# A graph layer on one core: window sums with carried overlaps, degree counts on two halves of the array, and tiles projected beside them

## The chip, the cores and the metric

The program runs on one core of a Trainium2 chip. The core has a matrix engine (PE in the profile; PEld is its weight load), a vector engine (DVE), a scalar engine (ACT), a general engine (POOL) and a queue engine (SP) that mostly issues transfers. The five follow their own instruction lists and meet at semaphores. The metric is the time of one execution in device microseconds (us), the median of the runs.

## The reference

There are 6250 nodes with 256 features and 200000 edges, which are sorted by their destination `dst`; many edges end at low node numbers, few at high ones. The reference does this:

```python
deg_out = clip(segment_sum(ones, src), 1)
deg_in  = clip(segment_sum(ones, dst), 1)
h  = feats * rsqrt(deg_out)[:, None]
m  = segment_sum(h[src], dst) * rsqrt(deg_in)[:, None]
x  = (m @ W_gc + b_gc) + (feats @ W_res + b_res)
core = moe(x)          # top 2 of 64 experts, 256 -> 512 -> 256, capacity 1024
y  = x + core          # then batch norm over the nodes, residual and layer norm
```

The change lies in all that comes before `x`, and in the one addition that forms `x`. The experts and the norms behind it stay as they are.

## The kernel before

**Projection first.** Since the sum over edges and `W_gc` commute, the kernel projects each of 50 tiles of 125 nodes with `W_gc` and `W_res` side by side (`wcat`, 512 columns): two transposes on PE into `pt` (L261), an ACT copy to `fT` (L263), two matmuls into `pr` (L266), ACT copies of the two halves to `y` (L267) and `xr` (L268). Per five tiles POOL adds the biases `bsum` to `xr` (L269), which is then written to `r_dram`.

**Degree counts.** `deg_out` is counted by matmuls. A source number is split into `hi = src // 125` and `lo = src % 125`. Edges stand in 1568 groups of 128, one edge per partition. For 32 groups at a time DVE makes the one-hot rows of `hi` (`hot_hi`, L233) and of `lo` (`hot_lo`, L237), as comparisons of two bf16 operands, and PE does one matmul per group into `degp`, 50 x 128 (L241). Both one-hot tiles have two buffers.

**Scaling and splitting.** With the counts there, `s_out` = 1/sqrt(degree) is formed. ACT scales `y` by it and rounds the result to the first half of `hrow` (L351); DVE puts what the rounding lost into the second half (L352). `hrow` is held on the chip and written to `h_dram` too, five tiles at a time on SP.

**Sums over edges.** The 1563 groups that hold edges are divided by a planner, `_plan()`. The first `GD` groups, where destinations are dense, form dense chunks of a tuple `(g0, k, w, n)`: `n` slots of `k` groups, each with at most `w` neighbouring destinations. For each group DVE makes a one-hot of `lo` (L410) and one of a combined key for (`hi`, slot position) (`hotk`, L414); PE multiplies them (L416), which counts how often each source meets each destination; ACT moves a slot's counts to `counts` (L418). When a chunk's counts are full, PE multiplies them with all 50 tiles of `hrow`, both halves (100 matmuls, L424 and L426). ACT copies the sums, and a one-hot matmul (`to`, L437, called spread) moves each sum to its place in a window of 128 nodes.
The other groups form gather chunks: POOL's indirect transfer fetches the 128 rows of a group from `h_dram` (L380) into a ring of `NR` = 10 buffers, DVE makes a one-hot of the destination within a window of 128 (`hot`, L383), and PE adds both halves (L384, L385) into the chunk's window.
Before, there are 35 dense chunks (997 groups) and 33 gather chunks (566 groups).
Windows of neighbouring chunks overlap, since a node's edges may stretch over two chunks. Each of the 68 windows is therefore added to `z_dram` by a POOL indirect transfer with addition (L361), some ten gathers after it was formed (`LAG`).

**What sets the order.** A scheduler orders the instructions of each engine by its own estimates, and the program's text sets what may pass what. In the sum phase the text runs both kinds of chunks side by side: before gather number `issued`, dense steps are taken until their planned cost reaches `share * (issued + 10)`. The `share` is the planned cost of all dense steps per gather, 648.9/566 = 1.146 before and 629.7/582 = 1.082 after. Counting only the costs that the steps themselves report (596 and 585), dense steps run out before gather 510 of 566, and in the changed kernel before gather 531 of 582.

**Keys.** The keys and tests which tell for every edge whether it fits its slot and window are made from `dst` and from tables of first destinations by some twenty POOL operations over 128 x 1568 or 128 x `GD` values (L294 to L334), with three of DVE (L325 to L327) that use `okd`, a flag that no degree is above 4096. Edges that fit nowhere are handled by a general loop behind the sum phase, which runs zero times for this input.

## Time and profile before

| quantity | value |
| --- | --- |
| median of 3 runs | 2521.09 us (2520.99 to 2524.98) |
| profiled execution | 2519.15 us, span from first to last instruction 2517.4 us |
| mean granted clock of PE | 0.847 |
| busy: PE, DVE, ACT, POOL | 1860.4, 1218.8, 543.8, 1151.8 us |
| first gather issued, last scatter issued | 468.45, 1382.76 us |
| bytes moved by transfers | 387.12 MB, mean 154 GB/s |

An instruction row reads: start, duration, engine, line, operation, output<-inputs, shape, count, and in brackets the idle time ahead of it with what ended it. A group row gives count, busy time, mean ns of one, and idle time with its releasers. A wait row gives the time waited in all, how often, and the longest. Ends of matmuls are modelled, so the distance of two starts says more than a duration. Matmuls on `hrow` are listed as f32.

### The profile page before, as it was taken

The page shows a single profiled execution, that of the slowest core. Times are in us where ns is not written, and L with a number is a line of the kernel's source. Part 1 is how long each engine was busy: PE and PEld are TensorE (multiplying, and loading weights), DVE is VectorE, ACT ScalarE, POOL GpSimd, SP SyncE. Part 2 cuts the span into 40 slices and gives each one's busy share as a digit, 9 for nine tenths or more (in the row PEclk, how much of TensorE's full clock was granted, in tenths as well). Part 3 has the DMA queues.
Part 4 walks back from the last instruction along what each step waited for, and adds up shares of the span by engine and source line. Part 5 has one row for each costly group of instructions (what it writes and reads, how often), then busy time and mean ns, then how long its engine had stood idle before and what let it go on. Part 6 is the DMA issues. An engine that isn't in the chain of part 4 may idle for free. (4 is left out here: it accounts for less than half of the span.)

```text
span 2517.4 us, 32629 instructions
## 1 busy us (share of the span) xinstructions
PE 1860.4 (74%) x10910; PEld 1413.1 (56%) x10910; DVE 1218.8 (48%) x4128; ACT 543.8 (22%) x1376; POOL 1151.8 (46%) x1097
## 2 busy tenths in 40 slices
PE   3808865989999999999884642679999999843340
PEld 3605421566777888878773530258888888730010
DVE  6907229766665555544431369931111112223368
ACT  0001224222433333333320210012222222310020
POOL 6992230476677777777767000022222222138800
PEclk9958985798899999999995555989999999975565
DMA  9501226376566666776676820057777777873314
GB/s 238 174 0 32 82 61 217 105 195 156 146 168 169 180 179 180 176 181 166 172 190 183 216 63 0 1 185 220 225 221 226 224 222 219 260 188 84 83 35 132
DMA packets 243599, 387.12 MB, mean 154 GB/s; under 512 B 29643, under 2 KB 172035, under 8 KB 243430
## 3 DMA queue, kind: packets, MB, share of 16 engines
q0 software_dynamic: 75360, 191.62, 29.7%
q1 hardware_dynamic: 128891, 153.92, 20.5%
q10 hardware_dynamic: 39179, 39.47, 5.5%
q8 instruction: 89, 1.46, 0.2%
q14 instruction: 80, 0.66, 0.1%
HBM read 304.86 MB, written 79.96 MB: 153 GB/s over the span
## 5 line engine op out<-in xcount | busy, mean ns | idle before, releaser
L380 POOL DMA_INDIRECT r<-h_dram,srcg x566 | 550.3, 972 | 222.6 <-issue 74.8
L424 PE MATMUL sm<-hrow,counts 125*126 125x258 f32 (+2 forms) x1750 | 436.9, 287 | 0.2
L426 PE MATMUL sm<-hrow,counts 125*126 125x256 f32 (+2 forms) x1750 | 434.5, 285 | 0.0
L679 POOL DMA_INDIRECT xg<-x_dram,ids x128 | 121.4, 948 | 619.7 <-PE pte L682 325.5
L383 DVE TENSOR_SCALAR hot<-iota_f,key 128x128 fp32r<-128x128 f32 x566 | 157.9, 303 | 397.0 <-PE pg L385 395.3
L424 PEld LDWEIGHTS sm<-hrow,counts 125*126 125x126 f32 (+2 forms) x1750 | 335.4, 192 | 1.1 <-issue 0.4
L426 PEld LDWEIGHTS sm<-hrow,counts 125*126 125x126 f32 (+2 forms) x1750 | 335.8, 192 | 0.0
L416 PE MATMUL pc<-hotk,lo 128*128 128x250 bf16 (+5 forms) x997 | 293.8, 329 | 49.0 <-DVE lo L410 25.3
L414 DVE TENSOR_SCALAR hotk<-iota_h,key 128x250 bf16<-128x250 f16 (+5 forms) x997 | 326.4, 330 | 0.0
L689 PE MATMUL ph<-xgT,w1s 128*128 128x256 f32 (+1 forms) x1280 | 274.8, 366 | 16.8 <-DVE xgT L684 16.8
L418 ACT CAST counts<-pc 128x350 fp32r<-128x350 f32 (+5 forms) x670 | 261.1, 489 | 111.8 <-PE pc L416 104.9
L410 DVE TENSOR_SCALAR lo<-iota_h,lo_f 128x128 bf16<-128x128 f16 x997 | 255.2, 257 | 25.1 <-PE pc L416 24.1
L696 PE MATMUL py<-w2s,hT 128*128 128x256 f32 x1152 | 262.0, 379 | 1.4 <-DVE ys L698 1.4
L689 PEld LDWEIGHTS ph<-xgT,w1s 128*128 128x128 f32 x1280 | 218.1, 190 | 63.1 <-DVE xgT L684 26.7
L698 DVE TENSOR_TENSOR ys<-py,b2s 128x256 f32<-128x256 f32 x144 | 60.9, 424 | 387.1 <-PE py L696 333.0
L384 PE MATMUL pg<-r,hot 128*128 128x258 f32 x566 | 199.4, 359 | 64.2 <-DMA r<-h_dram,srcg 48.1
L696 PEld LDWEIGHTS py<-w2s,hT 128*128 128x128 f32 x1152 | 217.5, 190 | 30.6 <-DVE ys L698 1.8
L691 ACT ACTIVATE hT<-ph,b1T 128x256 f32<-128x256 f32 x256 | 121.3, 474 | 364.2 <-PE ph L689 364.2
L416 PEld LDWEIGHTS <-lo 128*128 128x128 bf16 x997 | 91.9, 99 | 180.7 <-DVE hotk L414 75.3
L266 PE MATMUL pr<-wcat,fT 128*125 128x512 f32 x200 | 106.6, 667 | 97.8 <-ACT fT L263 97.8
L385 PE MATMUL pg<-r,hot 128*128 128x256 f32 x566 | 175.9, 316 | 0.0
L384 PEld LDWEIGHTS pg<-r,hot 128*128 128x128 f32 x566 | 114.7, 203 | 105.9 <-DVE hot L383 52.4
(219 smaller groups left out, 2180.2 us busy)
## 6 DMA issues: line engine op xcount, KB each, us to landing
w1s<-in_L_gnn_w_dram SPq DMA_DIRECT2D x80, 512.0 KB
w2s<-in_L_gnn_w_dram SPq DMA_DIRECT2D x80, 512.0 KB
y_dram<-ys SPq DMA_DIRECT2D x64, 256.0 KB
y_dram<-zeros ACTq DMA_DIRECT2D x1, 12416.0 KB
h_dram<-hrow SPq DMA_DIRECT2D x10, 1120.0 KB
b2s<-in_L_gnn_b_dram SPq DMA_DIRECT2D x80, 128.0 KB
r<-h_dram,srcg POOLq DMA_INDIRECT x566, 3.7
z_dram<-zeros ACTq DMA_DIRECT2D x1, 6321.0 KB
```

Source lines behind the costliest of these rows:

```text
L380: G.indirect_dma_start(out=f32(r[:, :2 * D]), out_offset=None, in_=h_dram[:, :], in_offset=bass.IndirectOffsetOnAxis(ap=idx, axis=0))
L383: V.tensor_scalar(hot, iota_f[:, :WIN], at, None, op0=ALU.is_equal)
L384: T.matmul(pg, hot, r[:, D:], start=first, stop=False)
L385: T.matmul(pg[:, :D], hot, r[:, :D], start=False, stop=last)
L410: V.tensor_scalar(lo, iota_h[:, :128], lo_f[:, g:g + 1], None, op0=ALU.is_equal)
L414: V.tensor_scalar(hot, iota_h[:, :NT * w], key[:, g:g + 1], None, op0=ALU.is_equal)
L416: T.matmul(pc, lo, hot, start=(i == 0), stop=(i == k - 1))
L418: S.copy(counts[:, :, j * w:(j + 1) * w], pc)
L424: T.matmul(sm[:m], counts[:TP, t, :m], hrow[:, t, D:], start=(t == 0), stop=False)
L426: T.matmul(sm[:m, :D], counts[:TP, t, :m], hrow[:, t, :D], start=False, stop=(t == NT - 1))
L689: T.matmul(ph[:, :m], w1s[:, kk, c * 128:(c + 1) * 128], xgT[:, kk, :m], start=(kk == 0), stop=(kk == 1))
L696: T.matmul(py, hT[:, c, k * 128:(k + 1) * 128], w2s[:, c, :], start=(c == 0), stop=(c == 3))
```

## The change

1. **Degree counts on two halves of the array.** `degp` has 128 partitions; even groups add into partitions 0 to 49, odd ones into 64 to 113 (L241, both before and after). The two halves are added when `s_out` is made.
2. **28 tiles projected beside them** (`EARLY`). They have no scale yet. ACT rounds the tile to `hrow` (L274), copies it unrounded to `whole` (L276, two buffers), and POOL writes the difference into `hrow`'s second half (L277). When `s_out` is known, POOL adds the two halves again (L358), and ACT (L251) and DVE (L252) scale and split anew. The remaining 22 tiles are projected after that and scaled straight from the accumulator `pr`. The buffer `y` and the pass over it are gone. Node tiles are read two at a time, not five, and `r_dram` is written from SP, not ACT. The bias addition moves to the stage that forms `x`.
3. **Keys.** A running maximum of the chunks' first destinations gives each window's base; ACT forms `mis` = `dst` - base in 68 pieces (L302, L303); the POOL operations follow on it (L315 to L338). `okd` is applied later, in `to` and in the general loop.
4. **Sweep with carried overlaps.** The windows of the dense chunks go upward, those of the gather chunks downward. Each window takes what its neighbour has for its nodes, by a one-hot matmul with the neighbour's copied result (`carried`, one-hot L424, `over`), and is then written over `z_dram` by a plain transfer on SP, whose row comes from a register (L431 to L433). POOL's 68 adding transfers go. The last dense window takes in both neighbours.
5. **One-hots of `lo` for eight groups at a time** (`PAIRS`) in the manner of the degree loop (L194), read by PE with a stride of two. `hotk` has ten buffers, not six; the ring of gathered rows has nine, not ten. The planner's costs change: 34 dense chunks (981 groups) and 34 gather chunks (582 groups).

The core of the diff:

```diff
+PAIRS = 8
+EARLY = 28
 FIRST = 256
 MORE = 2 * N // 128
 EXTRA = 16
-LAG = 10
...
     def cost(k, w, n):
-        return 13.0 + n * k * (0.06 + w * 0.0208)
+        return 13.5 + n * k * (0.04 + w * 0.0208)
 
     dense, g, pe = [], 0, 0.0
-
-    while pe + (NGU - g) * 0.33 < (NGU - g) * 1.25 + (len(dense) + 30) * 1.9:
+    while pe + (NGU - g) * 0.26 < (NGU - g) * 1.25 + 50.0:
...
-            c = cost(k, w, n) - 0.33 * n * k
+            c = cost(k, w, n) - 0.26 * n * k
...
-            srci = dp.tile([128, NGR], I32, name="srci")
-            nc.sync.dma_start(out=srci, in_=src)
-            dstf = dp.tile([128, NGR], F32, name="dstf")
-            G.dma_start(out=dstf, in_=dst)
-            mis = dp.tile([128, NGR], F32, name="mis")
-            G.dma_start(out=key, in_=bases[0:1, :].to_broadcast([128, NGR]))
-            G.dma_start(out=mis, in_=bases[1:2, :].to_broadcast([128, NGR]))
+            srcf = dp.tile([128, NGR], F32, name="srcf", tag="a")
+            G.dma_start(out=srcf, in_=src)
+            G.dma_start(out=key[:, :GD], in_=bases.to_broadcast([128, GD]))
+            first = dp.tile([128, NC], F32, name="first")
+            G.dma_start(out=first, in_=firsts.to_broadcast([128, NC]))
...
-                    T.matmul(degp, hot_hi[:, c // 2, :, c % 2], hot_lo[:, c // 2, :, c % 2],
-                             start=(c0 + c == 0), stop=(c0 + c == NGR - 1))
-
-
+                    r = c % 2
+                    T.matmul(degp[64 * r:64 * r + NT, :], hot_hi[:, c // 2, :, r],
+                             hot_lo[:, c // 2, :, r], start=(c0 + c < 2), stop=(c0 + c >= NGR - 2))
...
+            def halves(t, rows):
+
+                S.activation(hrow[:, t, :D], rows, AF.Copy, scale=s_out[:, t:t + 1])
+                V.scalar_tensor_tensor(hrow[:, t, D:2 * D], rows, s_out[:, t:t + 1],
+                                       f32(hrow[:, t, :D]), op0=ALU.mult, op1=ALU.subtract)
+                if t % 5 == 4:
+                    node_dma(nc.sync, False, f32(hrow[:, t - 4:t + 1, :2 * D]),
+                             node_rows(h_dram, t - 4, 5))
+
+            def project(t):
+                if t % 2 == 0:
+                    state["f"] = ld.tile([TP, 2, D], F32, name="f")
+                    node_dma(nc.sync, True, state["f"], node_rows(x_in, t, 2))
+                    state["xr"] = ld.tile([TP, 2, D], F32, name="xr")
+                f, xr = state["f"][:, t % 2, :], state["xr"]
+                pt = ps_a.tile([128, 2, TP], F32, name="pt")
+                for k in range(2):
+                    T.transpose(pt[:, k, :], f[:, k * 128:(k + 1) * 128], ident[:TP, :TP])
+                fT = ld.tile([128, 2, TP], F32, name="fT")
+                S.copy(fT, pt)
+                pr = ps_a.tile([TP, 2 * D], F32, name="pr")
+                for k in range(2):
+                    T.matmul(pr, fT[:, k, :], wcat[:, k, :], start=(k == 0), stop=(k == 1))
+                if t < EARLY:
+
+                    S.copy(hrow[:, t, :D], pr[:, :D])
+                    whole = ld.tile([TP, D], F32, name="whole")
+                    S.copy(whole, pr[:, :D])
+                    G.tensor_tensor(hrow[:, t, D:2 * D], whole, f32(hrow[:, t, :D]), ALU.subtract)
+                else:
+                    halves(t, pr[:, :D])
+                S.copy(xr[:, t % 2, :], pr[:, D:])
+                if t % 2:
+                    node_dma(nc.sync, False, xr, node_rows(r_dram, t - 1, 2))
...
+            for t in range(EARLY):
+                project(t)
...
+            V.tensor_tensor_scan(run, ones[:, :NC], first, 0.0, op0=ALU.mult, op1=ALU.max)
+            V.tensor_copy(base_i, run[0:1, :])
+            V.memset(shift, 0.0)
+            V.tensor_sub(shift[:, 1:ND], run[:, :ND - 1], run[:, 1:ND])
+            V.tensor_sub(shift[:, ND:NC], run[:, ND:NC], run[:, ND - 1:NC - 1])
+            V.tensor_scalar(shift, shift, pidx, None, op0=ALU.add)
+            neg = dp.tile([128, NC], F32, name="neg")
+            V.tensor_scalar(neg, run, -1.0, None, op0=ALU.mult)
+            mis = dp.tile([128, NGR], F32, name="mis", tag="b")
+            chunks = [(g0, k * n) for g0, k, w, n in DENSE] + GATHER
+            for c, (g0, k) in enumerate(chunks):
+                S.activation(mis[:, g0:g0 + k], dstf[:, g0:g0 + k], AF.Identity, bias=neg[:, c:c + 1])
...
+            G.tensor_tensor(key[:, :GD], dstf[:, :GD], key[:, :GD], ALU.subtract)
+            fit = dp.tile([128, NGR], BF16, name="fit")
+            t1 = dp.tile([128, NGR], BF16, name="t1")
+            G.tensor_scalar(fit, mis, 0.0, None, op0=ALU.is_ge)
+            G.tensor_scalar(t1, mis, float(WIN), None, op0=ALU.is_lt)
+            G.tensor_tensor(fit, fit, t1, ALU.mult)
...
+            V.tensor_copy(s_out, pd[:, :NT])
+            V.tensor_add(s_out, s_out, pd[:, 64:64 + NT])
...
+            for t in range(EARLY):
+                whole = ld.tile([TP, D], F32, name="whole")
+                G.tensor_tensor(whole, f32(hrow[:, t, :D]), f32(hrow[:, t, D:2 * D]), ALU.add)
+                halves(t, whole)
+            for t in range(EARLY, NT):
+                project(t)
...
-        for t in range(NT):
-            S.activation(hrow[:, t, :D], y[:, t, :], AF.Copy, scale=s_out[:, t:t + 1])
-            V.scalar_tensor_tensor(hrow[:, t, D:2 * D], y[:, t, :], s_out[:, t:t + 1],
-                                   f32(hrow[:, t, :D]), op0=ALU.mult, op1=ALU.subtract)
-            if t % 5 == 4:
-                node_dma(nc.sync, False, f32(hrow[:, t - 4:t + 1, :2 * D]),
-                         node_rows(h_dram, t - 4, 5))
...
-            NR = 10
+            NR = 9
...
-            def send(until):
-                while waiting and (until is None or waiting[0][0] <= until):
-                    _, res, idx = waiting.pop(0)
-                    add_to_nodes(res, idx)
+            def carried(pg, res, col, last):
+
+                to = rsp.tile([WIN, WIN], F32, name="over")
+                V.tensor_scalar(to, iota_f[:, :WIN], shift[:, col:col + 1], None, op0=ALU.is_equal)
+                T.matmul(pg, to, res, start=False, stop=last)
 
             def sums_done(pg, c):
...
-                res = rsp.tile([WIN, D + 2], F32, name="res", bufs=6)
+
+                res = rsp.tile([WIN, D + 2], F32, name="resd" if c < ND else "resg", bufs=2)
                 S.copy(res, pg)
-                waiting.append((issued + LAG, res, cidx[:, c:c + 1]))
+                row = nc.values_load(base_i[0:1, c:c + 1], engines=(SP_E,), min_val=0, max_val=N,
+                                     skip_runtime_bounds_check_because="at most N")
+                nc.sync.dma_start(out=z_dram[ds(row, WIN), :], in_=res)
+                return res
...
-                            lo = hc.tile([128, 128], BF16, name="lo")
-                            V.tensor_scalar(lo, iota_h[:, :128], lo_f[:, g:g + 1], None,
-                                            op0=ALU.is_equal)
+                            r = (g - g0) % PAIRS
+                            if r == 0:
+                                lo = hc.tile([128, PAIRS // 2, 128, 2], BF16, name="lo", bufs=3)
+                                hot_pairs(lo, lo_b, g, PAIRS, 128)
...
-                            T.matmul(pc, lo, hot, start=(i == 0), stop=(i == k - 1))
+                            T.matmul(pc, lo[:, r // 2, :, r % 2], hot, start=(i == 0), stop=(i == k - 1))
...
-                        T.matmul(pg, to[:m], sums[:m], start=True, stop=True)
-                        sums_done(pg, c)
-                spread()
-
-            steps, done = dense(), 0.0
+                        T.matmul(pg, to[:m], sums[:m], start=True, stop=(c == 0 and ND > 1))
+                        if c:
+                            carried(pg, ends_met["dense"], c, c < ND - 1)
+                        if c == ND - 1:
+                            carried(pg, ends_met["gather"], ND, True)
+                        ends_met["dense"] = sums_done(pg, c)
+                yield spread
...
+            for i, (g0, k) in reversed(list(enumerate(GATHER))):
                 pg = ps_g.tile([WIN, D + 2], F32, name="pg")
                 for g in range(g0, g0 + k):
-                    while steps is not None and done < share * (issued + 10):
-                        d = next(steps, None)
-                        if d is None:
-                            steps = None
+                    while finish is None and done < share * (issued + 10):
+                        d = next(steps)
+                        if callable(d):
+                            finish = d
                         else:
                             done += d
+                    alone = i == len(GATHER) - 1 and g == g0 + k - 1
                     gathered(pg, ring[issued % NR], srcg[:, g - GD:g - GD + 1], key[:, g:g + 1],
-                             g == g0, g == g0 + k - 1)
+                             g == g0, alone)
                     issued += 1
-                    send(issued)
-                sums_done(pg, ND + i)
-            for _ in steps or ():
-                pass
-            send(None)
+                if i < len(GATHER) - 1:
+                    carried(pg, ends_met["gather"], ND + i + 1, True)
+                ends_met["gather"] = sums_done(pg, ND + i)
+            while finish is None:
+                d = next(steps)
+                finish = d if callable(d) else None
+            finish()
...
             node_dma(nc.scalar, True, xr, node_rows(r_dram, t0, 5))
+            G.tensor_tensor(xr, xr, bsum[:, None, :].to_broadcast([TP, 5, D]), ALU.add)
             s_in = xl.tile([TP, 5], F32, name="s_in")```

Where instructions stand now. First POOL, between its last key operation and the first gathers (`r_...` are buffers of the ring). Before:

```order
L334 TENSOR_SCALAR mis<-mis 128x1568
L361 DMA z_dram<-res,cidx 6378x258
L380 DMA r_2956<-h_dram,srcg 128x512
L380 DMA r_2959<-h_dram,srcg 128x512
L380 DMA r_2962<-h_dram,srcg 128x512
```

After:

```order
L331 TENSOR_SCALAR key<-key 128x981
L337 TENSOR_SCALAR mis<-t_2648 128x587
L358 TENSOR_TENSOR whole<-hrow 125x256
L338 TENSOR_TENSOR mis<-mis,dstf 128x1568
L358 TENSOR_TENSOR whole<-hrow 125x256 x21
L414 DMA r_3184<-h_dram,srcg 128x512
L414 DMA r_3187<-h_dram,srcg 128x512
```

The scatter of the first dense window no longer stands ahead of the first gather; 21 of the 28 second additions now do, behind the key operations.

Second ACT, in the degree loop (tiles 2 and 3 of the projection). Before:

```order
L263 COPY fT<-pt 128x250 x2
L267 COPY y<-pr 125x256
L268 COPY xr<-pr 125x256
L267 COPY y<-pr 125x256
L268 COPY xr<-pr 125x256
```

After:

```order
L268 COPY fT<-pt 128x250 x2
L274 CAST hrow<-pr 125x256
L276 COPY whole<-pr 125x256
L280 COPY xr<-pr 125x256
L274 CAST hrow<-pr 125x256
L276 COPY whole<-pr 125x256
L280 COPY xr<-pr 125x256
```

Each tile has one ACT instruction more, and L276, which waits for POOL's subtraction of two tiles earlier, stands ahead of the next `fT`.

Third ACT after the degree loop, from the last small piece of `mis` to the first of the last sixteen tiles, in the changed kernel, with the rows between cut out at one place:

```order
L302 ACTIVATE mis<-dstf,neg 128x6
L353 ACT_TABLE_LOAD
L353 ACTIVATE s_out<-s_out 125x50
L314 ACTIVATE key<-mis 128x587
L251 ACTIVATE hrow<-whole,s_out 125x256 x2
L268 COPY fT<-pt 128x250 x2
...
L251 ACTIVATE hrow<-whole,s_out 125x256
L280 COPY xr<-pr 125x256 x2
L251 ACTIVATE hrow<-whole,s_out 125x256 x21
L268 COPY fT<-pt 128x250 x2
L251 ACTIVATE hrow<-pr,s_out 125x256
```

Between the small pieces and the 21 scalings only six tiles are projected; the other sixteen come behind the scalings, and so behind the POOL additions that these wait for.

226 lines of the change are left out of this document (100 added, 126 removed).

## The prediction

> **What bounds the kernel now.** I read the windows view first, cut at the borders of the stages, because the page's chain of waits begins only in the last 300 us. Columns: stretch, its length, then busy time of PE, PEld, DVE, ACT, POOL, TensorE clock, DMA share, GB/s.
>
> ```profile
> 32.00:263.00 231.00, 134.87 (x1629) 104.37 (x1628) 150.37 (x99) 16.09 (x47) 174.77 (x142) 0.83 0.30 88
> 267.00:362.00 95.00, 76.14 (x202) 34.45 (x203) 2.20 (x13) 30.80 (x102) 18.34 (x9) 0.93 0.29 80
> 362.00:386.00 24.00, 1.51 (x9) 0.76 (x9) 23.19 (x17) 2.68 (x8) 19.37 (x5) 0.58 0.18 61
> 411.00:466.00 55.00, 54.34 (x222) 26.48 (x222) 42.65 (x239) 10.94 (x29) 0.00 (x0) 0.60 0.45 141
> 466.00:900.00 434.00, 404.29 (x2564) 311.17 (x2564) 285.29 (x1347) 133.08 (x355) 305.67 (x294) 0.93 0.65 170
> 900.00:1100.00 200.00, 192.91 (x1398) 165.76 (x1398) 111.87 (x514) 77.28 (x213) 152.08 (x145) 1.00 0.70 179
> 1308.00:1382.00 74.00, 36.30 (x108) 25.11 (x108) 14.18 (x50) 1.78 (x5) 51.60 (x51) 0.55 0.78 201
> ```
>
> Four stages follow each other. To 263 us the degrees are counted, though DVE works for only 150 of the 231 us. To 362 PE projects. To 411 keys are finished and rows scaled, PE almost idle. From 411 to 1308 PE holds nearly all the time (dense counts and sums, gathers between them), and POOL has time to spare. To 1382 only gathers are left and POOL sets the pace. Behind that lie 1135 us which the change touches in one addition.
>
> Next I read the timeline and the waits of the first stage.
>
> ```profile
> 13.53 0.98 DVE L233 TENSOR_TENSOR hot_hi<-hi_b,iota 128x1600 bf16<-128x1600 bf16 x1
> 16.63 0.98 DVE L233 TENSOR_TENSOR hot_hi<-hi_b,iota 128x1600 bf16<-128x1600 bf16 x1
> 44.85 1.99 PE L241 MATMUL degp<-hot_lo,hot_hi 128*50 128x128 bf16 x32 [1.11 <-DVE hot_lo L237]
> 97.62 26.27 POOL L294 TENSOR_SCALAR cidx<-mis,pidx 128x1 int32<-128x1 f32 x10
> 214.14 13.61 POOL L269 TENSOR_TENSOR xr<-xr,bsum 125x1280 f32<-125x1280 f32 x1 [24.94 <-ACT xr L268]
> 276.66 2.89 POOL L269 TENSOR_TENSOR xr<-xr,bsum 125x1280 f32<-125x1280 f32 x1 [8.34 <-ACT xr L268]
> 300.39 3.70 PE L266 MATMUL pr<-wcat,fT 128*125 128x512 f32 x8 [0.58 <-ACT fT L263]
> 305.10 3.70 PE L266 MATMUL pr<-wcat,fT 128*125 128x512 f32 x8 [0.58 <-ACT fT L263]
> DVE hot_hi L233 <- PE degp L241: 92.8, 3, 67.5
> ACT y L267 <- POOL xr L269: 88.7, 4, 78.6
> ```
>
> One iteration of the loop (32 groups) costs DVE 3.10 us (13.53 to 16.63) and PE 1.99. While DVE runs these pairs POOL hardly moves: ten one-column operations took 26.27 us, and an addition of 13.61 us takes 2.89 alone. That late addition held ACT for 78.6 us in one wait, PE behind ACT, and DVE behind PE for 67.5. A projected tile costs PE half of 300.39 to 305.10, 2.35 us.
>
> **The change, stage by stage.** *Degree loop.* DVE can begin at about 15 (13.5 before; the source now comes by POOL's queue), so 49 x 3.10 = 152 us end at 167 if nothing stalls. Beside it PE has 49 x 1.99 + 28 x 2.35 = 163 us, almost as much, but 26 of the tiles stand in the last 30 iterations: there one iteration costs PE 1.99 + 0.87 x 2.35 = 4.03 against 3.10, which adds 30 x 0.93 = 28: 195. The POOL key operations and the 1280-column additions that jammed this loop are gone from it, but a new POOL subtraction per tile (L277) stands in the same place: the copy into `whole` waits for the subtraction two tiles earlier, and behind that copy wait ACT's transposed tiles, PE, and DVE. Its length is the 0.72 us of POOL's 125x256 addition to `bsum` (row further down), if POOL gets in. It does get in whenever DVE starves, so this locks itself together, it does not deadlock: per four tiles two subtractions (1.44), six ACT copies (0.40 each by the row of L351 below, 2.4), a tile on PE (2.35) and an iteration (1.99), 8.2 us, seven times, 57. So the end is between 195 and 15 + 152 + 57 = 224; I take 205, since PE is the slower side there anyway and DVE's own stalls hold part of the subtractions. Before: 263.
>
> The Trainium skill, "TensorEngine Tiling (Array Packing)", Key Properties, says that tiles of the array load and multiply in parallel, and the two halves are column tiles. The row of 44.85 shows one tile only. By that rule the 32 matmuls would take about half, 1.0 us, PE would need 3.04 per iteration, DVE would be the bound at 3.10, and the lockstep end of 224 would be the nearer one, not an earlier end.
>
> *From the counts to the first gather.* Groups of the by-shape view:
>
> ```profile
> L301 POOL TENSOR_SCALAR t<-key 128x1568 f32<-128x1568 f32 x1 | 4.2, 4217 | 0.0
> L302 POOL TENSOR_TENSOR fit<-fit,t 128x1568 f32<-128x1568 f32 x1 | 3.5, 3491 | 0.0
> L309 POOL TENSOR_SCALAR key<-key 128x997 f32<-128x997 f32 x1 | 2.7, 2722 | 0.1
> L307 POOL TENSOR_TENSOR wide<-wide,hi 128x997 f32<-128x997 f32 x1 | 2.3, 2292 | 0.0
> L351 ACT ACTIVATE hrow<-y,s_out 125x256 fp32r<-125x256 f32 x50 | 20.1, 493 | 21.5 <-PE pc L416 21.5
> L352 DVE SCALAR_TENSOR_TENSOR hrow<-y,s_out,hrow 125x256 fp32r<-125x256 f32 x50 | 20.2, 478 | 0.0
> L275 ACT COPY b1T<-pb 128x64 f32<-128x64 f32 x4 | 0.8, 213 | 0.2 <-PE pb L274 0.2
> L252 POOL TENSOR_TENSOR bsum<-bsum,bres 125x256 f32<-125x256 f32 x1 | 0.7, 723 | 18.5 <-DMA bres<-in_L_gnn_b_res_dram 18.5
> ```
>
> This work was hidden under the first 263 us; now it stands open. DVE's running maximum comes behind the loop, then 68 small ACT pieces of `mis` at some 0.21 us (L275's row is the nearest): 16 us with the start. Then POOL: 4 x 4.2 + 3 x 3.5 + 5 x 2.7 + 6 x 2.3 + 1.6 = 56, with seven L358 additions between them, 5: 77 us after the loop. Behind them 21 additions with their scaling in program order: 0.72 on POOL and 0.48 on DVE, one after the other, 25 us; ACT stands at them and does not feed PE. Then 16 tiles, PE-bound, 38, and 3 to drain. Sum 143: the last row of `hrow` is there at 205 + 143 = 348. Gone in return are the 95 us of projection, the 24 of keys and the 25 of scaling. Counts start on PE at 352 (411 before), gathers a few us later (468), since no scatter stands ahead of the first one.
>
> *Dense chunks beside gathers.*
>
> ```profile
> L380 POOL DMA_INDIRECT r<-h_dram,srcg x566 | 550.3, 972 | 222.6 <-issue 74.8 <-PE pg L385 74.0 <-PE pc L416 43.7
> L361 POOL DMA_INDIRECT z_dram<-res,cidx x68 | 113.0, 1662 | 115.5 <-ACT res L397 90.9 <-ACT counts L418 10.8 <-issue 8.8
> PEld L416 <- DVE hotk L414: 75.3, 196, 0.8
> PEld L416 <- DVE lo L410: 65.4, 156, 20.3
> PEld pg L384 <- DVE hot L383: 52.4, 80, 3.0
> 411.06 0.24 DVE L410 TENSOR_SCALAR lo<-iota_h,lo_f 128x128 bf16<-128x128 f16 x1
> 411.22 0.28 DVE L414 TENSOR_SCALAR hotk<-iota_h,key 128x250 bf16<-128x250 f16 x1
> 411.42 0.24 DVE L410 TENSOR_SCALAR lo<-iota_h,lo_f 128x128 bf16<-128x128 f16 x1
> 951.48 0.28 PE L384 MATMUL pg<-r,hot 128*128 128x258 f32 x1
> 951.72 0.28 PE L384 MATMUL pg<-r,hot 128*128 128x258 f32 x1
> 952.36 0.28 PE L424 MATMUL sm<-hrow,counts 125*126 125x258 f32 x1
> 952.48 0.28 PE L426 MATMUL sm<-hrow,counts 125*126 125x256 f32 x1
> 1307.89 0.70 PE L437 MATMUL pw<-sums,to 128*128 128x258 f32 x2
> 1377.32 0.98 POOL L380 DMA_INDIRECT r<-h_dram,srcg  x1 [0.30 <-issue]
> 1382.76 1.60 POOL L361 DMA_INDIRECT z_dram<-res,cidx  x1 [4.47 <-ACT res L397]
> ```
>
> At full pace a sum matmul is 0.12 us apart from the next (952.36, 952.48), a gathered group 0.24, a count matmul of some 330 columns 0.12 x 330/256 = 0.155, a spread 0.54 (its 0.70 less the 0.16 by which a 0.28 row exceeds its pitch of 0.12). Before: 35 x 100 x 0.12 + 997 x 0.155 + 510 x 0.24 + 35 x 0.54 = 716 us of work in the 897 from 411 to 1308: 181 lost, mostly where counts come in bursts and DVE makes one group in 0.36 us (411.06 to 411.42) against PE's 0.155. The three PEld rows put 193 us on DVE.
>
> After: 34 x 12 + 981 x 0.155 + 531 x 0.24 + (34 + 67) x 0.54 (spreads and carried overlaps) = 742. DVE saves 0.16 us of `lo` per group and pays one two-input operation of 1024 columns per eight: at the loop's 3.10 us for 1600 + 4096 columns that is 0.56, so 0.07 per group, 88 us less in all; and `hotk` may run ten groups ahead, not six. PE gains between nothing and all 88. I take half, 44, because bursts, not DVE's total, set the wait. Lost then: 137; 742 + 137 = 879, and the dense part ends at 352 + 879 = 1231. POOL needs 1.26 (0.97 and 0.30 of issue) x 540 = 680 us in that time and stays hidden, also without the 68 x 1.96 = 133 us of scatters, whose removal counts only in the tail.
>
> *Tail.* By the plan's shares 51 of 582 gathers remain when the dense steps run out (56 of 566 before); some nine are already in the ring, so 42 x 1.26 = 53 us instead of 1377.32 - 1307.89 = 69, the difference being the scatters. Last gather at 1284 instead of 1377. The last spread with its two carried matmuls, its copy and a plain write takes the place of copy and scatter (1377.32 to 1382.76): even. The x stage pays the ten moved additions on POOL, of which the first, 2.9 us, stands open: +3. What the carried windows wait for (their neighbour's copy) is a chunk old; the writes on SP have nothing behind them until z is read.
>
> **Sum**: -93 + 3 = -90. The profiled run took 2519.15 (span 2517.4), the median was 2 higher: 2519 - 90 = 2429, median 2431.
>
> **Rivals.** *A, PE gets all of DVE's 88 us* and the loop ends at 195: 44 + 10 less, 2377. For it: the 193 us of waits; against it: some loss is half clock (0.60 at 411 to 466).
>
> *B, no relief for PE*: bursts still wait on `hotk`, which keeps 0.20 per group; loss 181, 44 more: 2475.
>
> *C, POOL cannot get in, and every early tile stops DVE on its own*: subtraction 0.72, copies 1.2, PE 2.35, an iteration 1.99, 6.3 us x 28 = 176 instead of the 38 in the 205: +138, 2569, slower. It decides from (38 + 90)/28 = 4.6 us per tile. For it: the 13.61 us row. Against it: two `whole` buffers, and POOL finished there as soon as DVE ran dry.
>
> *D, the two-input `lo` holds up the gathers.* If it stopped POOL for each count burst of about 8 us, 34 x 8 = 272: POOL would need 680 + 272 = 952 instead of 879: 2504. Against it: most operations of a burst are the one-input `hotk` as before. [...]
>
> *E, the carried windows only move the scatter's cost*: SP's write waits and PE's fp32 matmuls cancel what setup gives; within 5 us of before.
>
> **How the numbers follow.** Forecast 0.45, A 0.20, B 0.16, C 0.07, D 0.09, E 0.03. The range 2368 to 2482 holds the forecast, A and B, 0.81. Faster by over 0.2% (5 us, what can be told from no change): 0.90; within it 0.03; slower, C, 0.07.
>
> **What would show it.** Right: (lines of the changed kernel) DVE's last `hot_lo` near 205, POOL's L277 in clumps of two where DVE pauses; the last L252 near 348; first L414 gather before 360; one chunk near 900 us in about 20 us; last gather near 1284. Wrong: L277 rows of 5 us or more throughout the loop (C); waits of L455 on `hotk` as large as now (B); gathers over 1.5 us beside `lo` (D); POOL's key operations far from 56 us.

## The result: 60 us faster, two thirds of the forecast

The changed kernel takes **2461.94 us** in the median (2457.15 to 2463.07, 4 runs) beside 2522.46 (2520.99 to 2524.98) for the kernel before in the same series: a ratio of 0.9755, 95% interval 0.9739 to 0.9772. That is -60.5 us. Forecast were -90, so the direction was right and the time lies within the range, nearest to rival B (2475, no relief for PE).

The marks of the two profiled executions, in us from the start of the span:

| mark | before | forecast | after |
| --- | --- | --- | --- |
| last degree one-hot ends | 262.8 | 205 | 188.5 |
| last row of `hrow` | 410.8 | 348 | 343.5 |
| counts start on PE (before: 15 groups already at 385.8) | 411 | 352 | 346.9 |
| first gather | 468.5 | before 360 | 351.8 |
| dense part ends | 1308 | 1231 | 1249 |
| last gather | 1377.3 | 1284 | 1303.6 |
| first row of `x` | 1393.3 | | 1326.7 |
| last logit | 1477.2 | | 1418.8 |
| end of the span | 2517.4 | 2427 | 2460.3 |

So the setup gave 64 us (59 forecast), the dense part gave nothing (902 us instead of 897, where 879 was forecast), the tail from there to the last gather took 54 us (53 forecast; 69 before), and the way from the last gather to the end grew from 1140.1 to 1156.7 us, by 17 where 3 was forecast.

The windows view of the changed kernel, cut at its own stage borders (columns as in the prediction):

```profile
19.00:189.00 170.00, 127.69 (x1710) 82.56 (x1712) 169.22 (x102) 33.90 (x111) 88.45 (x34) 0.88 0.58 158
204.00:259.00 55.00, 16.89 (x32) 7.07 (x32) 21.11 (x24) 11.12 (x28) 54.47 (x25) 0.66 0.13 37
259.00:344.00 85.00, 38.06 (x98) 17.26 (x98) 24.64 (x41) 28.61 (x69) 15.31 (x22) 0.70 0.58 176
500.00:900.00 400.00, 370.41 (x2596) 324.95 (x2595) 230.06 (x786) 131.94 (x376) 262.95 (x249) 0.95 0.62 174
900.00:1100.00 200.00, 180.81 (x1238) 163.04 (x1237) 92.01 (x297) 60.94 (x162) 118.96 (x114) 0.92 0.58 162
1249.00:1304.00 55.00, 32.77 (x96) 22.03 (x94) 14.52 (x48) 0.75 (x2) 41.59 (x45) 0.58 0.74 214
```

In the degree loop DVE is now busy without a gap (169.22 of 170). Then POOL is (54.47 of 55, the keys). From 259 to 344 nobody is: PE 38 of 85. And the row from 900 to 1100 has to be held against the same row of before: PE did 1398 matmuls there at clock 1.00, now 1238 at 0.92; POOL issued 145 operations, now 114.

**The late chunks.** A dense chunk consists of 100 sum matmuls and, until the next sums, a burst of counts with gathered groups among them (the rest). From the starts of the sums, chunk by chunk: counts start to the sums of the fourteenth chunk took 435 us before and 394 after, -41. From there to the last sum, 22 chunks took 461 us before, 21.0 each; 21 chunks take 506 after, 24.1 each (the last chunk of either has only its sums). Here is one of them in each kernel, before (first fence) and after (second): the windows row of the chunk and that of its rest, and ACT's copies of counts in the rest.

```profile
972.90:993.70 20.80, 19.99 (x148) 17.36 (x147) 11.04 (x51) 7.94 (x21) 16.23 (x16) 1.00 0.71 180
985.30:993.80 8.50, 7.69 (x45) 5.06 (x45) 7.95 (x37) 7.56 (x20) 6.67 (x7) 1.00 0.68 169
985.96 0.86 ACT L418 CAST counts<-pc 128x350 fp32r<-128x350 f32 x2
987.12 5.25 ACT L418 CAST counts<-pc 128x350 fp32r<-128x350 f32 x14
992.69 0.91 ACT L418 CAST counts<-pc 128x350 fp32r<-128x350 f32 x2 [0.31 <-PE pc L416]
```

```profile
918.90:944.20 25.30, 22.96 (x157) 20.89 (x155) 12.22 (x39) 7.81 (x21) 15.35 (x15) 0.90 0.56 151
933.20:944.20 11.00, 8.66 (x55) 6.59 (x54) 10.04 (x34) 7.81 (x21) 8.56 (x9) 1.00 0.69 175
933.84 1.24 ACT L457 CAST counts<-pc 128x350 fp32r<-128x350 f32 x3
935.45 4.90 ACT L457 CAST counts<-pc 128x350 fp32r<-128x350 f32 x13
940.63 0.86 ACT L457 CAST counts<-pc 128x350 fp32r<-128x350 f32 x2
```

These chunks have one group per slot, so every group needs an ACT copy, and 18 copies run almost back to back, 0.375 us apart (14 in 5.25): 7.6 us in both kernels, from 985.96 to 993.60 and from 933.84 to 941.49. A burst of 18 cannot be shorter than these copies. Before, the rest took little more (8.4 us here), with 11 gathered groups of PE inside it. DVE was as busy as ACT there (7.95 and 7.56 of 8.50), so these rows do not tell which of the two set the length. After, ACT is done at 941.5, but the next sums start at 944.2, and over all late chunks the rest takes 9.6 to 13.8 us, because 12 to 15 gathered groups stand in it and two at most among the sums. PE waits for their rows:

```profile
PE pg L418 <- DMA r<-h_dram,srcg: 58.0, 68, 2.5
PE pc L455 <- DVE hotk L453: 19.2, 30, 1.8
POOL r L414 <- PE sm L465: 59.5, 13, 8.0
1008.50 0.95 POOL L414 DMA_INDIRECT r<-h_dram,srcg  x1 [6.97 <-PE sm L465]
1009.75 0.95 POOL L414 DMA_INDIRECT r<-h_dram,srcg  x1 [0.30 <-PE pw L476]
```

(First three rows: the waits view from 347 to 1307 us; the wait for rows was 14.2 us in 17 pieces before.) POOL stops for 7 us while PE sums, since the ring is full and no gathered group is read among the sums; then it issues one every 1.25 us, and PE takes them as they land. The sums behind such a pause start at half pace: in 15 of the 21 late chunks, 11 to 26 of the 99 steps from one sum matmul to the next are over 0.2 us, not 0.12, and the row of this chunk has the clock at 0.90. Not all of the 3 us per chunk is waiting: about 1.4 gathered groups more (0.24 each) and nearly two carried products (0.44 each, by the starts of L425 and of the next matmul) are some 1.1 us of work, by estimate.

**What the pairs saved DVE.** One `lo` operation for eight groups has two prices in the changed kernel. The first row is of the source view (shortest, median and longest in ns), the others are of the timeline:

```profile
L194 DVE TENSOR_TENSOR lo<-lo_b,iota x135: 672/1206/1251, 345.8 to 1201.8; 128x1024 bf16<-128x1024 bf16 x135
810.14 0.68 DVE L194 TENSOR_TENSOR lo<-lo_b,iota 128x1024 bf16<-128x1024 bf16 x1
841.10 1.21 DVE L194 TENSOR_TENSOR lo<-lo_b,iota 128x1024 bf16<-128x1024 bf16 x1
```

In the seven chunks whose first group has an even number in the plan, all 41 operations took 0.67 to 0.69 us; in the 27 chunks with an odd first group, all 94 took 1.15 to 1.25, and e7 shows the same split. DVE's next operation starts 0.60 or 1.13 us later, so the 135 cost about 131 us, where 981 single ones at 0.16 would be 157: some 26 us saved, not 88. Nearly all of it lies in the even chunks, five of which are among the first fourteen. In a late chunk of 18 groups with an odd start, three operations (3.4 us) take the place of 18 (2.9 us): no relief at all. No run starts all chunks at even groups.

### The profile page after: what moved, and what is told of

Same layout as the page of the kernel before. It is cut to its first block, busy times and chain, and to the rows that moved or that the text cites. A ratio compares the mean times of both kernels' runs of the same rounds, so it can differ in the third digit from the quotient of the medians.

```text
span 2460.3 us, 32502 instructions
## 1 busy us (share of the span) xinstructions
PE 1809.5 (74%) x10958; PEld 1418.0 (58%) x10958; DVE 1229.5 (50%) x3405; ACT 553.0 (22%) x1435; POOL 1064.8 (43%) x960
## 5 line engine op out<-in xcount | busy, mean ns | idle before, releaser
L414 POOL DMA_INDIRECT r<-h_dram,srcg x582 | 608.3, 1045 | 415.0 <-PE pg L419 85.1
L463 PE MATMUL sm<-hrow,counts 125*126 125x258 f32 (+2 forms) x1700 | 444.4, 298 | 0.1
L465 PE MATMUL sm<-hrow,counts 125*126 125x256 f32 (+2 forms) x1700 | 438.5, 293 | 0.0
L463 PEld LDWEIGHTS sm<-hrow,counts 125*126 125x126 f32 (+2 forms) x1700 | 343.2, 202 | 1.7 <-ACT counts L457 0.8
L465 PEld LDWEIGHTS sm<-hrow,counts 125*126 125x126 f32 (+2 forms) x1700 | 342.4, 201 | 0.1
L745 PE MATMUL ph<-xgT,w1s 128*128 128x256 f32 (+1 forms) x1280 | 274.5, 365 | 18.1 <-DVE xgT L740 18.1
L453 DVE TENSOR_SCALAR hotk<-iota_h,key 128x250 bf16<-128x250 f16 (+5 forms) x981 | 256.3, 313 | 50.1 <-PE pc L455 48.5
L418 PE MATMUL pg<-r,hot 128*128 128x258 f32 x582 | 212.6, 369 | 81.7 <-DMA r<-h_dram,srcg 60.3
L457 ACT CAST counts<-pc 128x350 fp32r<-128x350 f32 (+5 forms) x654 | 249.9, 478 | 82.3 <-PE pc L455 73.6
L455 PE MATMUL pc<-hotk,lo 128*128 128x250 bf16 (+5 forms) x981 | 240.5, 317 | 23.8 <-DVE hotk L453 19.2
L418 PEld LDWEIGHTS pg<-r,hot 128*128 128x128 f32 x582 | 117.4, 202 | 128.8 <-DVE hot L417 51.0
L419 PE MATMUL pg<-r,hot 128*128 128x256 f32 x582 | 188.1, 326 | 0.0
L798 POOL DMA_INDIRECT yr<-y_dram,rowi x100 | 124.6, 1246 | 68.4 <-DMA y_dram<-ys 32.3
L194 DVE TENSOR_TENSOR lo<-lo_b,iota 128x1024 bf16<-128x1024 bf16 x135 | 141.4, 1048 | 0.0
L803 PE MATMUL pm<-x,ones 125*125 125x512 f32 x50 | 51.7, 1138 | 118.3 <-DVE x L800 98.4
```

What stands on the lines that cost most here:

```text
L414: G.indirect_dma_start(out=f32(r[:, :2 * D]), out_offset=None, in_=h_dram[:, :], in_offset=bass.IndirectOffsetOnAxis(ap=idx, axis=0))
L418: T.matmul(pg, hot, r[:, D:], start=first, stop=False)
L419: T.matmul(pg[:, :D], hot, r[:, :D], start=False, stop=last)
L453: V.tensor_scalar(hot, iota_h[:, :NT * w], key[:, g:g + 1], None, op0=ALU.is_equal)
L455: T.matmul(pc, lo[:, r // 2, :, r % 2], hot, start=(i == 0), stop=(i == k - 1))
L457: S.copy(counts[:, :, j * w:(j + 1) * w], pc)
```

## The experiments

They ran on chips of two kinds. On one the kernel before takes what it took above (2523.03; e5 to e8). On two others it takes 2663.36 (e1 to e4) and 2661.54 (e9 to e12). All ratios are to the kernel before on the same chip, and stage times are compared only between runs of one kind, called the first and the slower chip. The changed kernel without any edit ran on the first kind only; on the slower one e4 stands in for it.

**e5, the changed kernel again**, nothing edited.

> The changed kernel as it is, on the chip of the three runs beside it, so that they can be compared with it and not only with the kernel before: ratio to the kernel before 0.975 where the chip is like the first one; nearer 0.96 where gathers come late, as on the chip of e1 to e4.

2459.86, ratio 0.9745 (0.971 to 0.9779), with the last degree one-hot at 190.5, 894 us from the counts to the last sum (900 in the execution above), 1155.8 from the last gather to the end. Two executions of the same kernel thus differ by 6 us in the dense part. The ratio of 0.96 on the other kind came as expected (e4), but that gathers come late there is not shown: none of the traces of e1 to e4 has a landing time for a gather.

**e4, degrees on one half of the array.**

```diff
-                    T.matmul(degp[64 * r:64 * r + NT, :], hot_hi[:, c // 2, :, r],
-                             hot_lo[:, c // 2, :, r], start=(c0 + c < 2), stop=(c0 + c >= NGR - 2))
+                    T.matmul(degp[:NT, :], hot_hi[:, c // 2, :, r],
+                             hot_lo[:, c // 2, :, r], start=(c0 + c == 0), stop=(c0 + c == NGR - 1))
...
-            V.tensor_copy(dsb[64:64 + NT, :], degp[64:64 + NT, :])
```

> The changed kernel with the degree counts accumulated in one half of the array only (50 partitions), as before. If the two halves run at the same time on the chip, 32 matmuls take 2.0 us again instead of some 1.3, PE becomes the slower side where tiles are projected, and the degree loop ends 10 to 25 us later (near 205): 2470 to 2485. If the halves do not matter (DVE is the bound all through): within 5 us of 2462.

2561.83 on the slower chip, ratio 0.9622 (0.9601 to 0.9642); the loop ends at 188.7, as with two halves (188.5 to 195.2 in the runs with the same loop). Groups of the degree matmuls, before, after and e4:

```profile
L241 PE MATMUL degp<-hot_lo,hot_hi 128*50 128x128 bf16 x1563 | 99.1, 220 | 18.1 <-DVE hot_lo L237 18.1
```

```profile
L241 PE MATMUL degp<-hot_lo,hot_hi 128*50 128x128 bf16 x1568 | 65.8, 245 | 37.7 <-DVE hot_lo L194 32.9 <-DVE hot_hi L194 4.6
```

```profile
L241 PE MATMUL degp<-hot_lo,hot_hi 128*50 128x128 bf16 x1568 | 101.1, 222 | 22.1 <-DVE hot_lo L194 17.3 <-DVE hot_hi L194 4.5
```

The halves do overlap (busy 65.8 instead of 101.1 us), and it buys no time: PE waits for DVE in this loop either way (37.7 and 22.1 us). With one half, DVE waits 7.3 us for PE and only 20 of the 28 early subtractions fall into the loop, yet the last row of `hrow` comes no later (339.7).

**e3, no tile projected beside the counts.**

```diff
-EARLY = 28
+EARLY = 0
```

> EARLY = 0: no tile is projected beside the degree loop, all 50 are projected after it and scaled from the accumulator; no L277, no L358. If projecting early pays what the prediction counted, the degree loop ends near 171 instead of 188, and 50 tiles at 2.35 us after the small ACT pieces of mis end near 171 + 16 + 118 = 305, beside POOL's key operations (they end near 245): 40 us EARLIER than the 345 of the changed kernel, since the second additions, the scalings behind them and the reload of node tiles go. So 2415 to 2430. The rival (the early tiles are worth their 28 x 2.35 = 66 us of PE): 20 to 60 us later, 2480 to 2520.

2609.69 on the slower chip, ratio 0.9809 (0.9785 to 0.9833), 48 us slower than e4, as the rival had it. The loop ends at 172.0, so the early tiles and their subtractions cost the loop 17 us. That is DVE's own time: in the changed kernel 30 of its 98 operations are longer than the rest, by 16.2 us together, and here none is. But `hrow` was done only at 384.4, some 80 us later than the 305 worked out. PE's timeline of this run has them:

```profile
191.39 5.75 PE L271 MATMUL pr<-wcat,fT 128*125 128x512 f32 x8 [12.89 <-ACT fT L268]
233.65 3.39 PE L271 MATMUL pr<-wcat,fT 128*125 128x512 f32 x4 [24.66 <-ACT xr L280]
254.03 1.07 PE L266 MATMUL pt<-ident,f 125*128 125x125 f32 x4 [12.48 <-DMA f<-in_x_dram]
289.76 1.06 PE L266 MATMUL pt<-ident,f 125*128 125x125 f32 x4 [10.20 <-DMA f<-in_x_dram]
```

Node tiles are loaded on SP, behind the writes of `h_dram` and `r_dram` that wait for rows to be finished: four such waits of 10 to 12.5 us. The 24.66 was a wait of DVE: its `nmis` stands ahead of scalings and waits 25.5 us for POOL's keys. The changed kernel has the same on a smaller scale:

```profile
255.52 3.48 POOL L338 TENSOR_TENSOR mis<-mis,dstf 128x1568 f32<-128x1568 f32 x1
280.54 0.72 POOL L358 TENSOR_TENSOR whole<-hrow 125x256 f32<-125x256 f32 x1 [0.36 <-DVE hrow L252]
291.79 1.07 PE L266 MATMUL pt<-ident,f 125*128 125x125 f32 x4 [55.55 <-DMA f<-in_x_dram]
302.35 0.59 PE L266 MATMUL pt<-ident,f 125*128 125x125 f32 x4
317.31 1.06 PE L266 MATMUL pt<-ident,f 125*128 125x125 f32 x4 [10.27 <-DMA f<-in_x_dram]
```

POOL's last addition ends at 281.3, but PE's next tile starts at 291.79, and one more pause of 10.3 follows.

**e6, `r_dram` written from ACT's queue** (one edit of e7 too):

```diff
-  node_dma(nc.sync, False, xr, node_rows(r_dram, t - 1, 2))
+  node_dma(nc.scalar, False, xr, node_rows(r_dram, t - 1, 2))
```

> The changed kernel with r_dram written from ACT's queue again, not SP's. Theory Q (queue): the node tiles that are read on SP stand behind writes there which wait for scaled rows; in the changed kernel PE waited 10 us after the last scaling, and 10 us again ten tiles later. Taken off SP, the rows of hrow are complete 15 to 25 us earlier (near 325 instead of 344), and the whole is as much shorter than e5. Rival (the 16 tiles wait for the scalings anyway, the reads hide behind them): within 5 us of e5.

2454.95 on the first chip, ratio 0.973 (0.9702 to 0.9758), 5 us below e5 with overlapping intervals, which is the rival's number. From the end of the loop to the last row of `hrow` it takes 142.3 us instead of e5's 156.4: the SP queue was some 14 us of it. The loop ends 6 us later (196.2), so that 8 are left at the last row of `hrow`. The later end is one wait of DVE for PE of 12.6 us; e11, whose loop is not edited, has one of 9.5 and ends at 195.2, so the edit need not be the cause.

**e2, `lo` one group at a time, one input** (as the kernel before does it):

```diff
-  lo = hc.tile([128, PAIRS // 2, 128, 2], BF16, name="lo", bufs=3)
-  hot_pairs(lo, lo_b, g, PAIRS, 128)
+  lo = hc.tile([128, 128], BF16, name="lo")
+  V.tensor_scalar(lo, iota_h[:, :128], lo_f[:, g:g + 1], None, op0=ALU.is_equal)
...
-  T.matmul(pc, lo[:, r // 2, :, r % 2], hot, start=(i == 0), stop=(i == k - 1))
+  T.matmul(pc, lo, hot, start=(i == 0), stop=(i == k - 1))
```

> The changed kernel with the one-hots of lo made one group at a time again, by a one-input operation, as before; hotk keeps ten buffers. Theory K: DVE bounds only the first five or six chunks, which hold 390 groups; 0.09 us per group there, some 35 us more, little in the late chunks: 2490 to 2505. Rival R: the gathers become faster (0.97 instead of 1.05 us) and the late chunks shorter by 2 to 3 us each, which takes back what the early ones lose: 2430 to 2465.

2586.31 on the slower chip, ratio 0.9713 (0.9692 to 0.9734), 24 us slower than e4 on that chip. From the start of the counts to the sums of the fourteenth chunk it takes 451 us beside 427 of e4, and from there to the last sum 564 beside 569. So the pairs are worth some 24 us in the early chunks, about as much as DVE saves there by the rows above, and nothing in the late ones, where it saves nothing. (In the whole time the counts start 11 us later here and the end is 7 shorter, which was not followed up.) The gathers, in the changed kernel and here:

```profile
L414 POOL DMA_INDIRECT r<-h_dram,srcg x582 | 608.3, 1045 | 415.0 <-PE pg L419 85.1 <-issue 74.4 <-PE pc L455 72.7
```

```profile
L416 POOL DMA_INDIRECT r<-h_dram,srcg x582 | 562.6, 967 | 582.9 <-PE pg L421 233.5 <-PE pc L456 102.2 <-issue 91.0
```

Rival D's effect exists (1045 beside 967 ns, 46 us of POOL in all; 1038 in e4, on the chip of e2) and is far too small to decide.

**The order of PE's instructions: e1, e10, e7, e9.** The gathered groups stand in clumps because the scheduler put them there. With the edit below PE runs the sum phase in the order of the program's text, where gathered groups stand evenly among counts and sums. e1 and e10 are the changed kernel with that edit alone, on the two slower chips; e7 is e6 with that edit and the write of `mis_dram` moved from SP's queue to POOL's, on the first chip; e9 is the kernel before with the edit.

```diff
+            with tc.manual_schedule(engines={mybir.EngineType.PE}):
                 steps, done, issued, finish = dense(), 0.0, 0, None
...
```

The rest of the sum phase stands inside this block, unchanged.

> The changed kernel; in the sum phase the matrix engine alone takes its instructions in the order of the program's text, in which one gathered group stands behind every eight to ten sum matmuls; nothing else is edited. Theory K (clumps): in the changed kernel all 13 to 15 gathered groups of a chunk stand among its counts, so POOL stops with a full ring during the 12 us of sums and PE then waits for POOL; late chunks take 25 us instead of 21 to 22. Then this run loses POOL's waits of 5 to 8 us per chunk and the 21 late chunks get 2 to 4 us shorter each: 40 to 70 us less, 2395 to 2425. Rival R (contention: the two-input lo slows the gathers, the carried matmuls lengthen each chunk): their number is the same, so within 10 us of the changed kernel's 2462.

> The changed kernel with TensorE in program order in the dense and gather phase and nothing else. The two runs with the r writes on ScalarE's queue differed by 16.6 us for this order (and the mis write). Clump theory: 15 to 20 us below the changed kernel, near 2443, dense phase end near 1230 us, late chunks even at about 23 us. Rival (order worth nothing by itself): 2457 to 2463.

> e6, with mis_dram written from POOL's queue, and with the matrix engine in the order of the text in the sum phase, as in e1. Theory K (clumps): against e6 the 21 late chunks lose 1 to 4 us each, 40 to 70 us in all on a chip like the first one, more on a chip like that of e1. Rival R (contention on POOL and the carried matmuls): against e6 no change.

> The kernel before with one edit: in the dense and gather phase TensorE runs in the order in which the program writes its instructions, instead of the order that the scheduler chose. Beside e10 (the changed kernel with the same edit) it tells what the change is worth when both kernels have the same kind of order. Theory that the scheduler's order costs the changed kernel what the forecast lacks (gathered groups in clumps): this run near the time before (2500 to 2535), and e10 80 to 95 us below it, near the forecast of -90. Rival that the order has nothing to do with the missing part (TensorE simply gets too little of VectorE's relief): e10 stays 55 to 65 us below this run, as the changed kernel does below the kernel before.

| run | chip | us | ratio, interval | counts to last sum, us |
| --- | --- | --- | --- | --- |
| e5, changed | first | 2459.86 | 0.9745 (0.971 to 0.9779) | 894 |
| e6 | first | 2454.95 | 0.973 (0.9702 to 0.9758) | 890 |
| e7 | first | 2438.35 | 0.9664 (0.9637 to 0.9691) | 876 |
| e4 (own order) | slower | 2561.83 | 0.9622 (0.9601 to 0.9642) | 996 |
| e1 | slower | 2488.65 | 0.9341 (0.9316 to 0.9367) | 913 |
| e10 | slower | 2488.20 | 0.9352 (0.9329 to 0.9374) | 916 |
| e9, before | slower | 2615.36 | 0.9827 (0.9802 to 0.9852) | 986 |

On the first chip the order, with the moved write, gives 16.6 us (e6 to e7), less than the 40 to 70 expected; on the slower chips 73 (e4 to e1 on one chip, whose halves differ too) for the changed kernel and 46 for the kernel before. e1 and e10 were expected in times of the first chip. With the same kind of order in both, the change is worth 127 us there (e9 to e10), more than the 80 to 95 expected: 62 up to the start of the counts and some 70 in the dense part, less what the end gives back. So the clumps do cost the changed kernel, and more than the order costs the kernel before; but the 80 to 95 cannot be taken over to the first chip, where the kernel before was not run in program order. Why the scheduler's order costs over four times as much on a slower chip stays open: PE shows pauses ahead of counts there which the profile puts to "issue", that is to nothing that it shows (63.5 us in e4). Since no gather has a landing time in the traces of these chips, waits for gathered rows may be among them.

e7 beats both kernels, and its late chunks tell why it gains no more. The windows view of e7, from 900 us and of one chunk, a late burst's ACT copies and gathered groups by line, and a row of the waits view from 347 to 1307 us:

```profile
900.00:1100.00 200.00, 183.86 (x1294) 155.01 (x1293) 104.42 (x316) 63.71 (x170) 120.97 (x120) 1.00 0.60 168
1020.90:1044.20 23.30, 21.53 (x150) 18.04 (x150) 12.57 (x39) 7.47 (x19) 14.35 (x14) 1.00 0.59 167
L457 ACT CAST counts<-pc 128x400 fp32r<-128x400 f32 x16 | 6.5, 580 | 0.0
L418 PE MATMUL pg<-r,hot 128*128 128x258 f32 x3 | 1.2, 400 | 0.0
PE sm L463 <- ACT counts L457: 23.3, 33, 1.1
```

The clock is 1.00, PE waits for rows 20.7 us in the phase instead of 58.0, and the late chunks take 22.9 to 23.7 us: 14.3 to 15.1 for sums with 10 to 12 gathered groups between them, 8.3 to 9 for a burst with three to five. Now the gathered groups lengthen the sums by some 2.6 us (11 x 0.24), while the burst stays as long as ACT's copies make it (PE's sums wait for them, last row), with little of PE's to fill it. The kernel before, with 11 in the burst and two among the sums, took 21.0 us per chunk, 1.9 less than e7 (481 us for 21 chunks); some 1.1 of that is the work named above, so its order is better by some 0.8 us per chunk at most, as far as this shows. With 15 gathered groups per chunk about four would have to go among the sums. That order was not tried.

**e12, a ring of 12 buffers** instead of 9, in the scheduler's order.

```diff
-            NR = 9
+            NR = 12
```

> The changed kernel with a ring of 12 gathered buffers in place of 9, nothing else. Theory of the full ring (GpSimd fills nine buffers and stops while TensorE runs about 100 sums in a row, and TensorE then waits at GpSimd's pace of 1.25 us per gather): the late chunks fall by about three gathers' waits, 1 to 3 us in each of some 20 chunks, so the dense end 20 to 40 us earlier and the time 2420 to 2445. Rival (GpSimd's stop costs nothing, TensorE's own work sets the chunk): 2455 to 2464.

2563.7 on the slower chip, ratio 0.9652 (0.962 to 0.9684). Counts to last sum take 983 us, beside 988 in e11 and 996 in e4, which have nine buffers: at most 13 us, less than the expected 20 to 40. The chunks 14 to 22 were 2.8 us shorter than in e11 (25.4 and 28.2 on average), as the theory of the full ring has it, and the later ones lost that again. The time is no shorter than e4's. The theory is therefore not confirmed by the total: three buffers more do not undo what the clumps cost.

**e8, e7 without early tiles** (`EARLY = 0`).

> e7 with EARLY = 0. In e3 the degree loop ended at 172, as expected, but PE waited some 70 us for node tiles behind the writes on SP, and 25 us for ACT. With the writes off SP, theory Q: 50 tiles at 2.3 us after 188 end near 310, beside POOL's key operations, 15 us before e7: 15 us faster than e7. If projecting early is worth its place even so, hrow is complete later than in e7, and this run is 10 to 40 us slower than e7.

2462.0 on the first chip, ratio 0.9761 (0.9731 to 0.979), 24 us slower than e7. The loop ends at 171.7 and `hrow` is done at 361.9, not near 310: the waits behind SP's writes are gone, but DVE's `nmis` still holds up the scalings for 25.5 us until POOL's keys are ready. Without the early tiles the loop ends 23 us earlier than in e7 and `hrow` is done 20 us later; in all they are worth 24 us.

**e11, no bias addition in the x stage.** The expectation is wrong in one point: the biases of these inputs are not zero, so this kernel leaves out a part of `x`, and its routing is another one. It is read up to the logits.

```diff
-            G.tensor_tensor(xr, xr, bsum[:, None, :].to_broadcast([TP, 5, D]), ALU.add)
```

> The changed kernel without the bias addition of the x stage (GpSimd, ten times 2.9 us; both biases are zeros in these inputs, so the sum that is left out adds nothing). Theory that this moved addition is what makes the way from the last gather to the end 17 us longer than before: first x 3 us earlier, logits 8 to 10 us earlier after the first x, last gather to end of the span 1157 -> 1143 to 1147, the time 2447 to 2452. Rival (the stage is bound by the loads, which now come from ScalarE's queue together with z): no more than 3 us, 2458 to 2462.

2556.41 on the slower chip, ratio 0.9618 (0.9592 to 0.9645). Last gather to last logit: 99.9 us before, 115.2 after, 115.3 in e12 on the same chip as e11, 104.8 in e11. The addition is 10.5 of the 15 us. The groups of DVE's `x` operation before, after and in e11, and for the kernel after its source view and POOL's first and third additions:

```profile
L521 DVE SCALAR_TENSOR_TENSOR x<-z,s_in,xr 125x256 f32<-125x256 f32 x50 | 20.8, 478 | 0.2
```

```profile
L577 DVE SCALAR_TENSOR_TENSOR x<-z,s_in,xr 125x256 f32<-125x256 f32 x50 | 28.7, 628 | 5.3 <-POOL xr L571 4.7
1323.76 2.87 POOL L571 TENSOR_TENSOR xr<-xr,bsum 125x1280 f32<-125x1280 f32 x1 [19.25 <-DMA xr<-r_dram]
L577 DVE SCALAR_TENSOR_TENSOR x<-z,s_in,xr x50: 469/477/3110, 1326.7 to 1414.1; 125x256 f32<-125x256 f32 x50
1331.74 4.69 DVE L577 SCALAR_TENSOR_TENSOR x<-z,s_in,xr 125x256 f32<-125x256 f32 x5 [1.10 <-POOL xr L571]
1333.22 2.93 POOL L571 TENSOR_TENSOR xr<-xr,bsum 125x1280 f32<-125x1280 f32 x1 [1.51 <-DMA xr<-r_dram]
```

```profile
L576 DVE SCALAR_TENSOR_TENSOR x<-z,s_in,xr 125x256 f32<-125x256 f32 x50 | 21.0, 479 | 0.9 <-DMA xr<-r_dram 0.8
```

The later additions are not all hidden, though they overlap. The mean of 628 instead of 478 ns hides how: 47 of the 50 operations take 0.48 us as before, and three that start during an addition take 3.10, 3.11 and 2.74 us. DVE is busy 7.9 us longer with the 50 (28.7 beside 20.8). With the first 2.9 us, which stand open, that makes 10.8. The Trainium skill, "SBUF — State Buffer", "SBUF: two separate sides", says that a VectorE operation with two SBUF inputs and a GpSimd operation that reads SBUF exclude each other, each for its whole length. The rows agree: the fifth operation of the row at 1331.74 ends at 1336.43, just after the addition, which ends at 1336.15. The remaining 5 us (first `x` still 19.5 us after the last gather in e11, 16.0 before) was not settled.

## Why the prediction was right or wrong, step by step

- **Degree loop, end at 205: too late by 17.** The lockstep and the PE-bound iteration of 4.03 us did not come: 49 pairs of 3.10 us from 19.2, the 16.2 us by which 30 of DVE's operations are longer, and 0.7 of waiting for PE make up the loop. The two halves take a third off PE's busy time in these matmuls (65.8 us beside 101.1). The Trainium skill, "TensorEngine Tiling (Array Packing)", Key Properties, has tiles work in parallel, and the trace agrees; but the lockstep end of 224 that was called nearer by that rule did not come, and with one half (e4) the loop ends no later. Nor did rival C come. POOL's part of it is in these rows of the changed kernel:

```profile
32.65 44.63 POOL L315 TENSOR_TENSOR key<-dstf,key 128x981 f32<-128x981 f32 x1 [13.20 <-DMA dstf<-in_dst_dram]
75.38 2.75 DVE L194 TENSOR_TENSOR hot_hi<-hi_b,iota 128x1600 bf16<-128x1600 bf16 x1 [0.22 <-PE degp L241]
77.24 8.89 POOL L277 TENSOR_TENSOR hrow<-whole,hrow 125x256 fp32r<-125x256 f32 x5
116.83 1.17 POOL L277 TENSOR_TENSOR hrow<-whole,hrow 125x256 fp32r<-125x256 f32 x1 [2.47 <-ACT whole L276]
121.88 2.72 DVE L194 TENSOR_TENSOR hot_lo<-lo_b,iota 128x4096 bf16<-128x4096 bf16 x1
```

  POOL took 44.63 us for a 981-column subtraction (one of that size takes 2.21 behind the loop), while DVE ran its pairs back to back; it finished when DVE waited for PE for 0.22 us. After that the subtractions took 0.6 to 2.7 us, 1.2 in the median, and most of DVE's operations beside one were 0.4 to 0.6 us longer (2.72 beside 2.28). The early tiles in all cost the loop 17 us (e3 beside e4), not 57.
- **From the counts to `hrow`, 143: 155.** ACT's pieces of `mis` 15 us (16), the keys with five additions 55.4 (61, with seven; the other two ran in the loop), 21 additions 22 (25), tiles at 4.52 us per pair (4.70): each term slightly smaller than put. What failed is a term that was not there, the queue: node tiles behind the writes on SP, 21 us in two pauses. e6, with one of the two kinds of writes moved away, took 142. The prediction named SP's writes only in the tail, although the diff moved `r_dram` to that queue.
- **Dense part, 742 of work and 137 lost: 160 lost.** The term that failed first is DVE's relief of 88 us. It priced an operation for eight groups at 0.56 us, from the degree loop's rows; it takes 0.60 us in the chunks with an even first group and 1.13 in the 27 others, so that DVE saved some 26 us. "I take half, 44" was wrong too: where DVE saved, PE gained about all of it (24 us in the first fourteen chunks, e2 on the slower chip). The first thirteen chunks gave 41, near the 44 for the whole phase, but that is luck; where the other 17 came from (ten buffers of `hotk`, gathers from the start) was not separated. The second step that failed is that "bursts, not DVE's total, set the wait" was taken as one thing for all chunks. In the late ones there was no relief for DVE, and the gathered groups that no longer fit beside the counts, 15 for 13 per chunk, brought waits for their rows and half pace behind them: 3 us more per chunk, about 1.1 of it work. The order takes part of this back (e7). "POOL has time to spare" was wrong as well for these chunks: 145 operations with 152 us busy and some 0.30 of issue each fill 196 of the 200 us from 900 on, so POOL was near its limit before. The sign named for this part, one chunk near 900 us in about 20 us, came out at 25.3 in the row above. In program order (e7) the part takes 876 us.
- **Tail, 53 us:** 54. The scatters' price was right.
- **x stage, +3: +17.** The first addition was counted, and the other nine were called hidden; three of them hold up DVE (e11). Some 5 us stay open.
- **Rivals.** A did not come: there were no 88 us to get. B's condition, waits on `hotk` as large as before, did not hold (6.0 us in PE's row and 75.3 in PEld's before, 19.2 and 28.9 after), though its time is near. D: real and hidden. E is refuted.

## What to carry to other kernels

Price an operation that serves several groups at every start that it will have, not only at the ones of another loop. Work out the bound of a burst for each kind of chunk apart, and ask which engines' lists run back to back in it: here the saving on DVE was worth its time only in the chunks where DVE was relieved. Where a scheduler places one stream's work in the shadow of another's, a few items more than the shadow holds cost a wait and the clock behind it; look at where they stand. A step that is moved to another engine is not hidden just because it overlaps: compare the durations of the neighbour's operations beside it and without it, one by one and not by their mean, and list what stands behind each transfer that changes queue.
